# Sparse attention over lists: when the first q rows are normed, where one list tile is loaded and where the first gathers land

## The chip, the cores and the metric

The kernel runs on one core of a Trainium2 chip. The metric is the device time in microseconds (us) of one execution. The engines are named as in the profile: PE (TensorE), DVE (VectorE), ACT (ScalarE), POOL (GpSimd) and SP (SyncE, which here only issues transfers). Each engine takes its instructions in the order in which they stand in its own program.

## The reference

One graph attention layer with 4096 source rows x, 4096 target rows h_target, width 512, 8 heads of 64, and a 4096 x 4096 adjacency matrix of which about 0.4% is set. The masks and scales are ones and the biases zeros in these inputs.

```python
hs = layer_norm(h_source, ln1_scale, ln1_bias)
ht = layer_norm(h_target, ln1_scale, ln1_bias)
q = (ht @ Wq + bq).reshape(T, H, HD) / jnp.sqrt(jnp.float32(HD))
k = (hs @ Wk + bk).reshape(S, H, HD)
v = (hs @ Wv + bv).reshape(S, H, HD)
logits = jnp.einsum('thd,shd->hts', q, k)
logits = jnp.where(edge_mask[None] != 0, logits, NEG)
ctx = jnp.einsum('hts,shd->thd', jax.nn.softmax(logits, axis=-1), v).reshape(T, D)
ht = layer_norm(ht + ctx @ Wo + bo, ln2_scale, ln2_bias)
out = _layernorm(x + ht + jax.nn.gelu(ht @ W1) @ W2)
```

## The kernel before

The kernel uses that few edges are set. It makes, for every target row, a list of the source rows it is joined to, gathers those rows of k and v, and computes attention over the list alone. A second, general path stands behind a flag and isn't taken with these inputs.

**Work and tiles.** Rows go in tiles of 128, so there are 32 tiles of targets and 32 of sources. Four kinds of work are woven together.

- The *projection* (`project`) loads x two tiles at a time into ring slots 12 to 16, norms them on ACT, transposes them on PE, and for every source tile makes k and v (`source`): four matmuls of 128x512 for each half (L929), a copy from PSUM to the buffer `kvr` on ACT for each half (L931), and one write of 128 rows of k|v, 512 KB, to the DRAM table `kvd` (L935, from ACT's queue). For the last source tiles `kvr` is one of ring slots 8 to 10.
- The *lists* (`all_edges`, `edges`) read the adjacency matrix in quarters of 128 x 1024 integers, 512 KB, four to a target tile and 128 in all. I number them from 0: quarter 80 is the first of target tile 20. SP issues the load (L713, `quarter`), ACT turns it into 0/1 bytes and counts them (L728, the sign step), DVE multiplies by positions (L733) and takes maxima (L735). After a tile's fourth quarter DVE decodes the list (L742 to L759), and the candidates that remain are written out from SP (L766). `sort` orders the first 16 tiles' rows by the number of their edges; one step of it on DVE is L849. The sorted records are scattered to DRAM (L853, POOL).
- The *front* of a target tile (`front`) makes its q: POOL has fetched the tile's record (L979, `prefetch`) and gathers its rows of h_target (L966 into `tq`). Then come the tie (L994) and the copy of tags (L997) on DVE, the norm on ACT (L998), four transposes on PE (L1002), four ACT steps (L1005), four matmuls with Wq (L1011) and a DVE step (L1016).
- *Attention* (`attention`) takes up to three list entries at once. POOL gathers 128 rows of k|v for each entry (L966 into `kv`, 512 KB), DVE multiplies by q (L1220) and adds up each head (L1225), ACT takes the exponential (L1229, or L1238 for a tile's first entries), DVE and ACT scale v (L1184, L1204), and PE transposes and accumulates (L1192). A finished tile goes on to the output projection (L1115) and the feed-forward part (`feed`: L1325, L1328, L1334), which fills PE for most of the run.

**The ring.** `ring` has 20 slots of 128 x 4 KB that change their use. While lists are made beside the projection, slots 0 to 7 hold list quarters, quarter n in slot n % 8, for the first NA + FILL = 16 + 5 tiles; 8 to 11 hold rows of h_target (their moments are taken early); 12 to 16 hold x. Slots 17 and 18 are the two "wide" buffers, which take turns: they serve the sort and the list quarters of all later tiles, so a load there waits until the sign step two quarters earlier is done. Slot 19 is scratch. In attention the gathers go round slots 0 to 16 (`place`, worked out when the program is built), later 0 to 19.

**What sets the order.** The Python generators are woven by costs written in the code (`_weave`), and a scheduler then orders each engine's instructions. Since it could place a front early, the tie is a data dependence put there on purpose: L994 reads a column of a tile in the list `latest` and writes the norm factors back unchanged, so that a front can't be placed before that tile is written. For the first fronts (`first_fronts`, two tiles, EARLY = 2) `latest` holds the first column of a `kvr` buffer of projection step n >= 14, that is, of one of the last four source tiles. Later it holds a column of the logits.

The first gather of k|v waits until all of `kvd` is written.

Of the kernel before, what the change touches and what calls it, by code (L numbers as in the profile page):

```python
# [423 lines left out]
def _take(gen, n):  # L424

    for _ in range(n):
        cost = next(gen, StopIteration)
        if cost is StopIteration:
            return
        yield cost  # L430
# [13 lines left out]
def adj_resnorm_kernel(  # L444
# [34 lines left out]
    N, D = x.shape  # L479
# [3 lines left out]
    NT = N // P  # L483
    G = 2
# [3 lines left out]
    NQ = 4  # L488
# [12 lines left out]
    NA, NBT = len(CAPS_A), len(CAPS_B)  # L501
# [31 lines left out]
    with tc.tile_pool(name="keep", bufs=1) as keep:  # L533
# [17 lines left out]
        with ExitStack() as late:  # L551
# [22 lines left out]
            def turn_of(name, places):  # L574
                turns[name] += 1
                return places[turns[name] % len(places)]
# [127 lines left out]
            adjs = []  # L704
            DEEP = 8
            FILL = 5

            def quarter(i, h):
                if i < NA + FILL:
                    a = ring[:, (i * NQ + h) % DEEP, :].bitcast(I32)  # L710
                else:
                    a = turn_of("wide", wide)
                nc.sync.dma_start(a, adj[i * P:(i + 1) * P, h * QW:(h + 1) * QW])  # L713
                return a

            def edges(i):

                part = 1 if i >= NA else 0
                rec = Rs[part][:, i - PARTS[part][0], :]
                cand = lp.tile([P, SEG, 8], U16, name="cand", bufs=2)  # L720
                for h in range(NQ):
                    n = i * NQ + h
                    while len(adjs) < min(n + 2, NT * NQ):
                        adjs.append(quarter(*divmod(len(adjs), NQ)))
                    a, adjs[n] = adjs[n], None

                    sg = turn_of("signs", signs)
                    nc.scalar.activation(sg, a, AF.Sign, accum_out=dpart[:, i, h:h + 1])  # L728
                    ahead = min(n + DEEP - 1, n + 3 + n // 2)
                    while len(adjs) < min(max(n + 3, min(ahead, (NA + FILL) * NQ)), NT * NQ):  # L730
                        adjs.append(quarter(*divmod(len(adjs), NQ)))
                    wd = sg.bitcast(U16)
                    nc.vector.tensor_tensor(wd, wd, lio, ALU.mult)  # L733
                    for s, (w0, w1) in enumerate(SEGS):
                        nc.vector.max(cand[:, h * SQ + s, :], wd[:, w0:w1])  # L735
                    if h == 1:
                        keep_rest()
                    if h % 2 and moms:
                        moments(moms.pop(0))
                    yield 2.0  # L740
                dec = dec_w
                nc.vector.tensor_single_scalar(dec[:, 0], cand, 255, op=ALU.bitwise_and)  # L742
                nc.vector.tensor_single_scalar(dec[:, 1], cand, 8, op=ALU.logical_shift_right)
                gid = lp.tile([P, 2 * SEG, 8], F32, name="gid")
                dec = dec.rearrange("p b s e -> p (b s) e")
                off = segoff.rearrange("p b q s -> p (b q s)")
                nc.vector.scalar_tensor_tensor(gid, dec, 0.0,
                                               off.unsqueeze(2).to_broadcast([P, 2 * SEG, 8]),
                                               op0=ALU.is_gt, op1=ALU.mult)
                nc.vector.tensor_add(gid, gid, dec)  # L750
                flat = gid.rearrange("p s e -> p (s e)")
                for r in range(RE // 8):
                    top = rec[:, E0 + r * 8:E0 + (r + 1) * 8]
                    nc.vector.max(top, flat)
                    if r + 1 < RE // 8:
                        nc.vector.match_replace(flat, top, flat, 0.0)
                held.append((rest_d[i * P:(i + 1) * P, :], flat))
                has = lp.tile([P, MAXE], F32, name="ehas")
                nc.vector.tensor_scalar(has[:, :RE], rec[:, E0:E0 + RE], 0.0, 0.0, op0=ALU.is_gt,  # L759
                                        op1=ALU.add, accum_out=cnt[:, i:i + 1])  # L760
                yield 4.0

            def keep_rest():

                while held:
                    nc.sync.dma_start(*held.pop())  # L766
# [21 lines left out]
            def all_edges():  # L788
                for i in range(NT):
                    yield from edges(i)  # L790
# [9 lines left out]
            def moments(i):  # L800

                while asked and len(asked) > NT - 4 - i:
                    ask(asked.pop(0))
                t = hrow(i)
                stats(ip, t, mvh[:, i, :], "n0")
# [58 lines left out]
            def project(order, t=None):  # L864
# [54 lines left out]
                def source(n, j):  # L919
                    g, hT = order[n], state[n][1]  # L920
                    if asked or moms:
                        kvr = sp.tile([P, 2 * D], F32, name="tq", bufs=3)
                    else:

                        kvr = ring[:, 8 + (n * G + j) % 3, :]
                    for half, w in enumerate((wk, wv)):
                        pkv = psi.tile([P, D], F32, name="pq", bufs=3)
                        for kc in range(KC):
                            nc.tensor.matmul(pkv, hT[:, kc, j * P:(j + 1) * P], w[:, kc, :],  # L929
                                             start=kc == 0, stop=kc == KC - 1)  # L930
                        nc.scalar.copy(kvr[:, half * D:(half + 1) * D], pkv)  # L931
                    if n >= 14:
                        latest[:] = [kvr[:, 0:1]]
                    r0 = 1 + (g * G + j) * P
                    newest[:] = [nc.scalar.dma_start(kvd[r0:r0 + P, :], kvr).ins]  # L935
                    return 7.8
# [26 lines left out]
            recs, tqs, h2Ts, done, ready, latest, newest = {}, {}, {}, set(), [], [], []  # L963
# [6 lines left out]
            def prefetch(i):  # L970
                if i >= NT or i in recs:
                    return
                r0 = TILES[i][0]
                part = 1 if r0 >= PARTS[1][0] * P else 0
                assert part in done
                r0 -= PARTS[part][0] * P
                rec = sp.tile([P, E0 + MAXE], I32, name="rec", bufs=6)

                nc.gpsimd.dma_start(rec[:, :RW], recs_d[part][r0:r0 + P, :])  # L979
                recs[i] = rec  # L980
# [39 lines left out]
            EARLY = 2  # L1020
# [1 line left out]
            SG = [(i, j0, min(S, cap - j0)) for i, (_, cap) in enumerate(TILES)  # L1022
                  for j0 in range(0, cap, S)]
            kvs, rests, fronts = {}, {}, {}
            place = [0]
            for i, _, n in SG:
                if place[-1] + n > RING[i >= NA]:
                    place[-1] = 0
# [6 lines left out]
            def step(gens, i):  # L1035

                if i in gens and next(gens[i], StopIteration) is StopIteration:
                    del gens[i]
# [111 lines left out]
            def go_on():  # L1150
                for i in list(fronts):
                    step(fronts, i)

            def first_fronts():

                for i in range(EARLY):
                    prefetch(i)
                for i in range(EARLY):
                    fronts[i] = front(i)
                    step(fronts, i)  # L1160
                while not latest:
                    yield None
                while fronts:
                    go_on()
                    yield 4.0
# [235 lines left out]
            def prepare():  # L1401

                yield from _take(ed, NA * steps)
                ready.append("lists")
                while moms:
                    moments(moms.pop(0))
                rs, nm = rstd_of(wp, mvh, NT, "n0")
                for R, (i0, n) in zip(Rs, PARTS):
                    Rf = R.bitcast(F32)
                    nc.vector.tensor_copy(Rf[:, :, RST], rs[:, i0:i0 + n])  # L1410
                    nc.vector.tensor_copy(Rf[:, :, RST + 1], nm[:, i0:i0 + n])
                nm = turn_of("wide", wide)
                nc.sync.dma_start(nm[:NT, :P], nodemask.rearrange("(c p) -> c p", p=P))
                nmf = nm.bitcast(F32)[:NT, P:2 * P]
                nc.vector.tensor_scalar(nmf, nm[:NT, :P], 1.0, None, op0=ALU.not_equal)
                nc.vector.tensor_reduce(bad[:NT, 0:1], nmf, AX.X, ALU.max)
                yield from sort(0)
                yield from first_fronts()

            def fill():  # L1420
# [3 lines left out]
                yield 9.0  # L1424
                for cost in _take(ed, FILL * steps):
                    yield cost
# [60 lines left out]
```

## Time and profile before

| | us |
|---|---|
| median of 3 runs | 1821.21 (1814.98 to 1824.7) |
| the profiled execution | 1811.19 |
| its span in the trace | 1809.4 |
| PE busy | 1681.5 (93%) |
| DVE busy | 1435.1 (79%) |
| ACT busy | 1221.1 (67%) |
| POOL busy | 979.8 (54%) |
| last k|v copy (L931) starts | 289.38 |
| first k|v gather (L966) starts | 296.81 |
| first attention product on DVE (L1220) starts | 308.02 |

How to read the views that follow. The page gives each engine's busy time, and the span cut into 40 slices of 45 us, where a digit is a busy share in tenths; PEclk is the clock granted to PE, in tenths of full speed, and DMA the mean busy share of the core's 16 DMA engines. A table of windows gives, for each stretch: its length, the busy us of PE, PEld (weight loads), DVE, ACT and POOL with the number of instructions, then PE's clock, the DMA share and GB/s. A list in order of time gives start, duration, engine, line, operation, output and input, and in brackets how long the engine had been idle and what released it. Such a releaser is inferred: where the engine named had long been done, it was another, often a transfer. For a transfer the duration is that of its issue; its landing is asked for separately. A matmul of 32-bit numbers is two records, so four matmuls show as x8.

### The profile page before, as it was taken

To read this page: it belongs to the slowest core of one execution; us is meant where nothing else is said; L and a number is where in the kernel's file an instruction comes from. 1 tells how busy PE (TensorE), PEld (TensorE's weight loads), DVE (VectorE), ACT (ScalarE), POOL (GpSimd) and SP (SyncE) were. 2 spreads that over 40 slices of the span, in tenths; PEclk is the share of its full clock that TensorE was granted. 3 is DMA by queue.
4 is the path that set the end of the run, shared out by engine and by line. 5 is a ranking of instruction groups with operands and counts; after the bars stand their busy time and mean duration, and the time that the engine had idled before them with its cause. 6 is when DMAs were issued, how large, how long until landed. Compare 5 with 4: busy or idle time off the path is not lost. (4 is left out here: it accounts for less than half of the span.)

```text
span 1809.4 us, 22969 instructions
## 1 busy us (share of the span) xinstructions
PE 1681.5 (93%) x7030; PEld 1101.4 (61%) x7030; DVE 1435.1 (79%) x2660; ACT 1221.1 (67%) x3119; POOL 979.8 (54%) x834
## 2 busy tenths in 40 slices
PE   7989984587999989999999989999999999999997
PEld 3434432465766666676776757666666666666664
DVE  6989886899999837777879989979879797988200
ACT  5767654486997636767768867877777676787211
POOL 1000144666566576667767788877575665663101
PEclk9999996698999999999999999999999999999998
DMA  9999968988887647778879888787776777774000
GB/s 343 370 376 375 344 228 293 405 276 321 294 300 237 230 159 258 240 253 279 281 256 320 288 263 292 252 281 261 242 273 216 255 239 247 247 246 149 18 6 26
DMA packets 140268, 463.26 MB, mean 256 GB/s; under 512 B 16500, under 2 KB 21672, under 8 KB 140136
## 3 DMA queue, kind: packets, MB, share of 16 engines
q0 software_dynamic: 96656, 342.64, 55.9%
q1 hardware_dynamic: 35664, 95.98, 15.0%
q10 hardware_dynamic: 7816, 23.08, 3.3%
q8 instruction: 58, 0.95, 0.2%
q14 instruction: 74, 0.61, 0.1%
HBM read 430.75 MB, written 30.89 MB: 255 GB/s over the span
## 5 line engine op out<-in xcount | busy, mean ns | idle before, releaser
L966 POOL DMA_INDIRECT kv<-kvd,rec x603 | 761.1, 1262 | 366.9 <-PE cps L1192 147.8
L1334 PE MATMUL po<-w,gt 128*128 128x512 f32 x1024 | 466.9, 598 | 10.3 <-ACT gt L1328 10.3
L1325 PE MATMUL pf<-h2T,w 128*128 128x256 f32 (+1 forms) x2176 | 466.5, 368 | 0.0
L1325 PEld LDWEIGHTS pf<-h2T,w 128*128 128x128 f32 x2176 | 389.7, 191 | 64.4 <-issue 19.8
L1220 DVE TENSOR_TENSOR kv<-kv,tq 128x1536 f32<-128x1536 f32 (+2 forms) x211 | 352.0, 1677 | 62.0 <-DMA kv<-kvd,rec 57.9
L1204 ACT ACTIVATE kv<-kv,pa 128x64 f32<-128x64 f32 x1520 | 390.9, 337 | 4.5
L1225 DVE TENSOR_REDUCE lg<-kv 128x24 f32<-128x1536 f32 (+2 forms) x211 | 350.4, 1668 | 1.2
L1334 PEld LDWEIGHTS po<-w,gt 128*128 128x128 f32 x1024 | 189.1, 192 | 207.2 <-issue 195.3
L1192 PE MATMUL cps<-ident,kv 128*128 128x128 f32 x2008 | 267.8, 282 | 47.7 <-DVE kv L1184 40.0
L1192 PEld LDWEIGHTS cps<-ident,kv 128*128 128x128 f32 x2008 | 242.2, 146 | 114.0 <-DVE kv L1184 45.8
L1184 DVE TENSOR_TENSOR kv<-kv,p 128x1024 f32<-128x1024 f32 (+1 forms) x211 | 251.3, 1195 | 23.8 <-ACT p L1229 22.5
L687 POOL TENSOR_TENSOR n_rs<-n_ve,mhalf 128x2 f32<-128x2 f32 (+2 forms) x51 | 48.6, 953 | 326.0 <-DVE n_ve L680 173.0
L728 ACT ACTIVATE kv<-kv 128x1024 uint8<-128x1024 int32 x128 | 134.9, 1055 | 94.5 <-DMA kv<-in_adj_dram 42.9
L1328 ACT ACTIVATE gt<-pf 128x512 f32<-128x512 f32 x128 | 76.3, 597 | 87.4 <-PE pf L1325 84.0
L1328 ACT ACT_TABLE_LOAD x103 | 132.1, 1283 | 1.7
L735 DVE MAX8 cand<-kv 128x8 uint16<-128x103 uint16 (+1 forms) x640 | 132.4, 253 | 0.5
L929 PE MATMUL pq<-wk,h2T 128*128 128x512 f32 x256 | 121.3, 619 | 8.3 <-ACT tq L931 5.7
L1229 ACT ACTIVATE p<-lg 128x24 f32<-128x24 f32 (+2 forms) x179 | 39.1, 218 | 120.5 <-DVE lg L1225 119.7
L1011 PE MATMUL t<-wq,tq 128*128 128x512 f32 x256 | 115.7, 595 | 2.1 <-ACT tq L1005 2.1
L929 PE MATMUL pq<-wv,h2T 128*128 128x512 f32 x256 | 115.4, 593 | 1.8 <-DVE rbc L662 1.0
L1115 PE MATMUL t<-wo,rb 128*128 128x512 f32 x256 | 115.2, 592 | 0.0
L929 PEld LDWEIGHTS pq<-wk,h2T 128*128 128x128 f32 x256 | 49.4, 199 | 65.3 <-issue 50.5
(160 smaller groups left out, 1581.8 us busy)
## 6 DMA issues: line engine op xcount, KB each, us to landing
kv<-in_adj_dram SPq DMA_DIRECT2D x128, 512.0 KB, 7.1
kvd<-tq ACTq DMA_DIRECT2D x24, 512.0 KB, 6.6
kv<-kvd,rec POOLq DMA_INDIRECT x603, 5.9
kv<-in_L_gnn_h_target_dram SPq DMA_DIRECT2D x32, 256.0 KB, 8.0
kv<-in_x_dram SPq DMA_DIRECT2D x15, 512.0 KB, 9.3
rest_d<-gid SPq DMA_DIRECT2D x32, 160.0 KB, 4.7
w<-in_L_gnn_W_dram SPq DMA_DIRECT2D x4, 1024.0 KB, 9.9
kvd<-kv ACTq DMA_DIRECT2D x8, 512.0 KB, 5.2
```

Of the source, the lines that this page charges most:

```text
L728: nc.scalar.activation(sg, a, AF.Sign, accum_out=dpart[:, i, h:h + 1])
L735: nc.vector.max(cand[:, h * SQ + s, :], wd[:, w0:w1])
L929: nc.tensor.matmul(pkv, hT[:, kc, j * P:(j + 1) * P], w[:, kc, :], start=kc == 0, stop=kc == KC - 1)
L966: nc.gpsimd.indirect_dma_start(out=dst, out_offset=None, in_=table[:, :], in_offset=bass.IndirectOffsetOnAxis(ap=idx, axis=0))
L1184: nc.vector.tensor_tensor(v4, v4, p[:, j0:j0 + m, :].unsqueeze(3) .to_broadcast([P, m, H, HD]), ALU.mult)
L1192: nc.tensor.matmul(cps[:, c, :], kv[:, j, D + c * P:D + (c + 1) * P], ident, is_transpose=True, start=j0 + j == 0 and c == 0, stop=j0 + n ...
L1204: newest[:] = [nc.scalar.mul(v, v, pa[:, hd:hd + 1]).ins]
L1220: nc.vector.tensor_tensor(kv[:, :n, :D], kv[:, :n, :D], tq[:, :D].unsqueeze(1).to_broadcast([P, n, D]), ALU.mult)
L1225: nc.vector.tensor_reduce(lg[:, :n, :], kv[:, :n, :D].rearrange("p j (h d) -> p j h d", h=H), AX.X, ALU.add)
L1325: nc.tensor.matmul(pf[:, k, :], w1[(f0 + k) // KC][:, kc, (f0 + k) % KC * P:((f0 + k) % KC + 1) * P], h2T[:, kc, :w], start=kc == 0, stop= ...
L1328: nc.scalar.activation(gt, pf, AF.Gelu_apprx_tanh)
L1334: nc.tensor.matmul(po[j], gt[:, k, j * P:(j + 1) * P], w2[(f0 + k) // KC][:, (f0 + k) % KC, :], start=False, stop=f0 + k == FC - 1, skip_g ...
```

## The change

It has four parts. `latest` is filled only at the last source tile, with the first column of the second half (v) of its `kvr`, so the first fronts are tied to the end of the projection. The constant RINGED = NA + FILL - 1 takes the place of NA + FILL where list quarters are placed and loaded ahead: the quarters of tile 20 (80 to 83) use the two wide buffers instead of ring slots 0 to 3. `place` starts at 11 instead of 0: the first two groups of gathers go to slots 11 to 16 and the third to slots 0 to 2. In `first_fronts` the two loops become one, so that each tile's record is fetched just ahead of the start of its front.

```diff
             DEEP = 8
             FILL = 5
+            RINGED = NA + FILL - 1
 
             def quarter(i, h):
-                if i < NA + FILL:
+                if i < RINGED:
                     a = ring[:, (i * NQ + h) % DEEP, :].bitcast(I32)
                 else:
                     a = turn_of("wide", wide)
...
                     ahead = min(n + DEEP - 1, n + 3 + n // 2)
-                    while len(adjs) < min(max(n + 3, min(ahead, (NA + FILL) * NQ)), NT * NQ):
+                    while len(adjs) < min(max(n + 3, min(ahead, RINGED * NQ)), NT * NQ):
                         adjs.append(quarter(*divmod(len(adjs), NQ)))
...
                         nc.scalar.copy(kvr[:, half * D:(half + 1) * D], pkv)
-                    if n >= 14:
-                        latest[:] = [kvr[:, 0:1]]
+                    if n * G + j == NT - 1:
+                        latest[:] = [kvr[:, D:D + 1]]
...
             kvs, rests, fronts = {}, {}, {}
-            place = [0]
+            place = [11]
             for i, _, n in SG:
...
                 for i in range(EARLY):
                     prefetch(i)
-                for i in range(EARLY):
                     fronts[i] = front(i)
                     step(fronts, i)
```

## The prediction

> **What bounds the kernel now.** I read the page's busy table and its 40 slices first, then a table of windows, then each engine's list in order of time between 240 and 320 us, and last the landing times of single transfers.
>
> ```profile
> PE 1681.5 (93%) x7030; PEld 1101.4 (61%) x7030; DVE 1435.1 (79%) x2660; ACT 1221.1 (67%) x3119; POOL 979.8 (54%) x834
> ...
> PE   7989984587999989999999989999999999999997
> ...
> PEclk9999996698999999999999999999999999999998
> DMA  9999968988887647778879888787776777774000
> ```
>
> PE is the bound, with one hole: slices 6 to 8 (271 to 407 us), between the k|v projection and full attention. The windows give its size:
>
> ```profile
> 260.00:280.00 20.00, 11.77 (x28) 5.61 (x27) 9.65 (x45) 6.19 (x11) 11.21 (x14) 0.74 0.64 194
> 280.00:300.00 20.00, 12.26 (x28) 4.86 (x26) 12.02 (x52) 11.02 (x23) 2.58 (x3) 0.92 0.74 240
> 300.00:320.00 20.00, 2.82 (x12) 2.42 (x12) 13.74 (x24) 6.83 (x21) 14.86 (x15) 0.50 1.00 387
> 320.00:340.00 20.00, 8.66 (x32) 6.29 (x32) 17.05 (x24) 7.12 (x28) 12.70 (x10) 0.50 1.03 402
> ...
> 440.00:1750.00 1310.00, 1278.47 (x5635) 878.63 (x5636) 1056.01 (x1362) 936.11 (x2496) 830.74 (x686) 0.99 0.72 240
> ```
>
> From 440 us PE is busy 97.6% of the time, so what starts attention earlier by some microseconds ends the kernel earlier by about as much, unless it is lost before 440. From 300 to 340 the DMA share is full: the gathers themselves set the pace. Before 300 it is 0.64 and 0.74, so there is room. The lists in order of time show who waits in the hole (start, duration, work, idle time before it and its releaser):
>
> ```profile
> 268.84 0.22 DVE L994 SCALAR_TENSOR_TENSOR rec<-rec,kv 128x2 f32<-128x2 f32 x1 [6.78 <-DMA rec<-rec]
> ...
> 273.06 0.81 ACT L998 ACTIVATE tq<-tq,rec 128x512 f32<-128x512 f32 x1 [9.30 <-DVE gid L750]
> ...
> 273.93 1.11 PE L1002 MATMUL t<-ident,tq 128*128 128x128 f32 x4 [7.91 <-ACT tq L998]
> ...
> 289.38 0.62 ACT L931 COPY kv<-pq 128x512 f32<-128x512 f32 x1
> 290.03 0.33 ACTq L935 DMA_DIRECT2D kvd<-kv  x1
> ...
> 296.81 0.96 POOL L966 DMA_INDIRECT kv<-kvd,rec  x1 [20.42 <-ACT kv L728]
> ...
> 308.02 1.77 DVE L1220 TENSOR_TENSOR kv<-kv,tq 128x1536 f32<-128x1536 f32 x1 [1.98 <-DMA kv<-kvd,rec]
> ...
> 314.89 2.82 PE L1192 MATMUL cps<-ident,kv 128*128 128x128 f32 x12 [22.14 <-DVE kv L1184]
> ```
>
> The first two q fronts stand in the middle of the projection. Their tie (L994) waits for records, their ACT step (L998) for the tie and a gather; behind L998 stand five k|v copies (L931), behind L1002 the last row's 16 k|v matmuls. The last copy ends at 290.0, its write lands 6.0 us after issue, at 296.05, and the first gather follows at 296.81. The 20.42 us put down to L728 are not a wait for a slot: slots 0 to 2 held list quarters 80 to 82, whose signs ended by 248.7. The releaser is the k|v write.
>
> **What the skill says.** "Trainium Kernel Development and Optimization", Key Constraints: DMAs from SP, ACT and POOL share the same 16 DMA engines and interleave. The trace agrees: with list loads, weights and gathers together, a gather's landing grows from 7.3 us (issued 296.8) to 16.9 (issued 319.3). "DMA: Bandwidth & Descriptors", Anatomy of one DMA: 2.0 us plus bytes/436e3, which estimates 3.2 us for a 512 KB list quarter. The trace has 3.8 at best and 5.5 as median of 235 to 300 us; I use the trace. "TensorE: Matmul & The Clock Gate", Part 1: the clock is halved after an idle window of about 3.4 us. It agrees: 0.50 from 300 to 340.
>
> **The tie moved.** No instruction but two ACT table loads (1.28 us each, on an engine 67% busy) is added: nothing. In the built order the last row's matmuls stand ahead of both L1002 groups, all copies ahead of L998, and L994 behind the sign step of quarter 92. The 9.30 us on ACT, 7.91 on PE and 6.78 on DVE go. But fourteen sign steps still stand among the copies as before, quarters 79 to 92, and the last copy still stands behind quarter 92. So the list loads decide when the last copy runs.
>
> **The fifth list tile outside the ring.** Quarters 80 to 83 now use the two wide slots. Quarter 81 waits on SP for the sort's L849, as quarter 85 did before (issued 242.27, landed 3.8 later); the rest-of-list writes and loads behind it on SP wait too. From 82 on each load waits for the sign step two quarters earlier. Quarter 81 is signed at 246.5 to 247.6 as before, 80 ends at 246.6, so 82 is issued at 246.7 and 83 at 247.8. Then the even chain 82, 84, ... 92 has six landings and five turns of 1.35 us (sign 1.06, accumulator 0.19, issue 0.1). Landings before: 3.8, 6.3, 4.6 as given, and 5.4, 5.0, 4.0 where a sign step waited for its load: mean 4.85. The three with two loads in flight average 5.6. I take 5.2: 246.7 + 6 x 5.2 + 5 x 1.35 = 284.65; sign 1.06, copy 0.57: the last copy ends at 286.3, not 290.0. PE isn't later: the last half row needs the copy three halves before, due near 272.6, and ends near 276. DVE needs 1.34 us for a quarter (0.41 + 0.93) and 4.1 for a tile's decoding, 2.4 a quarter against 3.3 of the loop.
>
> **The first gathers.** Write issued 286.4, landing 5.5 (before: 4.3, 5.2, 6.0), 0.75 to the first gather: 292.6 against 296.81. The third is issued 2.5 later and lands after 8.2 as before: 303.3, so L1220 starts at 303.8 against 308.02, 4.2 earlier. Slots 11 to 13 instead of 0 to 2 give nothing, as shown above; the cover is the write's landing. Ahead of them on POOL stand two gathers of x that need L997's tags. These move from 274 to about 287 and 288, still 4 us before the k|v gathers; if the copy were much later they would move with it.
>
> **The fronts.** Tie and tags end at 287.1; L998 twice to 288.7; eight transposes to 290; L1005, eight at 0.36, to 291.7; L1011, 7.13 for both, first tile done at 294; L1016 behind a list quarter on DVE at 294.5. All of it, some 8 us, is hidden by the gathers' flight until 303.3, with 8.8 to spare. Without that cover it would cost up to 8.
>
> **First softmax.** Before, L1225 ended at 311.85 but the exponential waited until 313.38, since ACT first signed quarter 98 (312.32). In the new order only quarters up to 96 stand ahead of it; 96 lands near 302. With the second L1016 (0.6) in between, L1225 ends at 307.8 and L1238 follows: 5.5 earlier.
>
> **What comes back.** Two list quarters fewer are done ahead of the first softmax; the built order catches up at about the 17th gather group, at 385 to 400 us of the old trace. That is 2 x 1.34 + half a decode of 4.1 = 4.7 us of DVE, 2.5 of ACT, 1 MB of loads. DVE waits 7 us for gathers from 300 to 345, which can hide it, but from 380 to 400 it is 19.56 of 20 busy. Bounds 0 and 4.7; I take half, 2.3. POOL once waits for a prefetched record (landing 5.6 us, two issues before it), where it later waited 3.3 and 3.6 for PE: nothing. The ring's reuse distance stays 5 to 7 groups: nothing.
>
> **Sum.** 5.5 - 2.3 = 3.2 us earlier: the profiled execution's 1811.2 (span 1809.4) would become 1808.0. That execution lies 10 below the median shown, 1821.2; the same 3.2 from the median gives 1818.
>
> **The rivals.**
> Likeliest, as above, with loads landing in 4.4 to 6.6 us: between 8 faster and 8 slower, 1813 to 1829. Chance 0.58. For it: the last copy is merely moved from one waiting chain to another.
> *Faster*: the loads land in 4.2 on average, since no pair is held up by the record scatters that ended at 263.5. The chain is 6.0 shorter, and the deferred quarters hide in DVE's waits: 5.5 + 6.0 = 11.5 faster, less a little for the full DMA engines: 1811. For it 3.8, 4.0 and 4.6; against it 6.3 with two in flight. Chance 0.22.
> *Slower*: the two-slot loop becomes the bound of the projection's end. At 7.0 us a landing the last copy ends at 297.1, the gathers start 6.6 later than before, the softmax some 5.3 later, and the deferred quarters cost all 4.7: 10.0 slower, 1831. With 2.3 for them the loss begins at 5.7 us; with 4.7 it passes 0.5% at 6.85. For it: medians of 6.3 from 240 to 330 us and 7.4 once gathers run; against it: DMA shares of 0.54 to 0.74 in that stretch. Chance 0.20.
> That the slots change nothing is already in the likeliest case. If the wait named L728 had been a real slot wait, the write at 296.05 would still hold the gathers.
>
> **How the numbers follow.** 0.5% of 1821 is 9.1 us, about what a measurement of this kernel can tell from no change. Faster by more: 0.22. Slower by more: 0.20. Within: 0.58. The time is the likeliest case's 1818; its own range is 1813 to 1829. From 1808 to 1831 it takes in most of both other cases and leaves the outer parts, 2 in 10 with the runs' own spread (1815 to 1825).
>
> **What would show it.** Right: no ACT stall ahead of L998 but short ones ahead of L728; PE goes from L929 to L1002 without projection behind it; last L931 near 286; first k|v gather near 292 to 293; first L1220 near 304; first L1192 near 309. Wrong: the last copy at 290 or later with L728 waiting for list loads (the slower case), or before 281 (the faster one); an L1016 that ends after the gathers have landed; DVE list work between 380 and 400 ahead of an idle PE.

## The result

The changed kernel takes 1817.42 us in the median (1813.57 to 1822.71), the kernel before 1818.92 (1810.74 to 1824.7), 20 executions of each on one chip. The ratio is 0.9994, with a 95% interval of 0.9983 to 1.0005: no difference that the runs can show, and the 1818 that was predicted. The profiled execution after the change took 1817.49 us (span 1815.5).

The page of the changed kernel, busy times and slices as in the prediction:

```profile
PE 1677.8 (92%) x7030; PEld 1097.9 (60%) x7030; DVE 1436.5 (79%) x2660; ACT 1224.1 (67%) x3121; POOL 982.2 (54%) x834
...
PE   7989984597999979999999989999999999999997
...
PEclk9999996698999989999999999999999999999998
DMA  9999968989887557777878878787776776774000
```

The hole in slices 6 to 8 stands on PE at 4, 5 and 9 tenths, where it stood at 4, 5 and 8. The table of windows says how it moved inside (length, busy us of PE, PEld, DVE, ACT, POOL, then PE's clock, DMA share, GB/s):

```profile
260.00:280.00 20.00, 13.92 (x31) 5.83 (x32) 12.22 (x51) 8.82 (x17) 8.91 (x12) 1.00 0.75 231
280.00:300.00 20.00, 7.97 (x17) 3.93 (x16) 11.55 (x52) 11.75 (x25) 4.93 (x5) 0.57 0.78 246
300.00:320.00 20.00, 7.11 (x22) 3.97 (x21) 13.26 (x19) 6.91 (x22) 15.38 (x15) 0.74 1.02 398
320.00:340.00 20.00, 5.64 (x24) 4.84 (x24) 14.47 (x23) 4.71 (x18) 12.09 (x10) 0.51 1.03 402
```

PE's busy time over the four windows is 34.64 us, where it was 35.51. The order changed as predicted. The lists of the changed kernel in order of time (the lines between 708 and 1158 have one number more than before; L995 is the old L994, L932 the old L931, and so on):

```profile
266.11 0.58 ACT L932 COPY kv<-pq 128x512 f32<-128x512 f32 x1 [3.95 <-remote]
...
288.93 1.06 ACT L729 ACTIVATE kv<-kv 128x1024 uint8<-128x1024 int32 x1 [2.57 <-DMA kv<-in_adj_dram]
...
289.99 0.57 ACT L932 COPY kv<-pq 128x512 f32<-128x512 f32 x1
...
291.03 1.52 ACT L999 ACTIVATE tq<-tq,rec 128x512 f32<-128x512 f32 x2 [0.48 <-DVE rec L995]
...
291.90 1.97 PE L1003 MATMUL t<-ident,tq 128*128 128x128 f32 x8 [11.28 <-ACT tq L999]
...
296.58 0.94 POOL L967 DMA_INDIRECT kv<-kvd,rec  x1 [3.00 <-DMA rest_d<-gid]
...
308.06 1.76 DVE L1220 TENSOR_TENSOR kv<-kv,tq 128x1536 f32<-128x1536 f32 x1 [5.18 <-DMA kv<-kvd,rec]
...
313.65 2.82 PE L1192 MATMUL cps<-ident,kv 128*128 128x128 f32 x12 [9.36 <-issue]
```

The long wait ahead of the norm (L999) is gone, and ahead of the last copies stand short waits for list loads at the sign steps (L729). On PE the wait wasn't removed but moved: 11.28 us ahead of L1003, at a place where PE has nothing else to do. Yet the last copy starts at 289.99 (before 289.38) and the first product at 308.06 (before 308.02): in this execution attention starts when it always did. So two questions were open. Why did the start stay, and would an earlier start have been worth anything?

### The profile page after: what moved, and what is told of

Its sections match the earlier page's. It is cut to its first block, busy times and chain, and to the rows that moved or that the text cites. A ratio compares the mean times of both kernels' runs of the same rounds, so it can differ in the third digit from the quotient of the medians.

```text
span 1815.5 us, 22973 instructions
## 1 busy us (share of the span) xinstructions
PE 1677.8 (92%) x7030; PEld 1097.9 (60%) x7030; DVE 1436.5 (79%) x2660; ACT 1224.1 (67%) x3121; POOL 982.2 (54%) x834
## 5 line engine op out<-in xcount | busy, mean ns | idle before, releaser
L1325 PE MATMUL pf<-h2T,w 128*128 128x256 f32 (+1 forms) x2176 | 465.9, 368 | 0.1
L1325 PEld LDWEIGHTS pf<-h2T,w 128*128 128x128 f32 x2176 | 389.3, 191 | 64.5 <-issue 20.3
L1220 DVE TENSOR_TENSOR kv<-kv,tq 128x1536 f32<-128x1536 f32 (+2 forms) x211 | 351.6, 1675 | 68.3 <-DMA kv<-kvd,rec 56.2
L1225 DVE TENSOR_REDUCE lg<-kv 128x24 f32<-128x1536 f32 (+2 forms) x211 | 350.1, 1666 | 1.4
L729 ACT ACTIVATE kv<-kv 128x1024 uint8<-128x1024 int32 x128 | 134.9, 1056 | 100.0 <-DMA kv<-in_adj_dram 51.7
```

The source lines that it names most:

```text
L1220: nc.vector.tensor_tensor(kv[:, :n, :D], kv[:, :n, :D], tq[:, :D].unsqueeze(1).to_broadcast([P, n, D]), ALU.mult)
L1225: nc.vector.tensor_reduce(lg[:, :n, :], kv[:, :n, :D].rearrange("p j (h d) -> p j h d", h=H), AX.X, ALU.add)
L1325: nc.tensor.matmul(pf[:, k, :], w1[(f0 + k) // KC][:, kc, (f0 + k) % KC * P:((f0 + k) % KC + 1) * P], h2T[:, kc, :w], start=kc == 0, stop= ...
```

## The experiments

Every ratio is to the kernel before, run on the same chip beside it. The table holds what the experiments turn on: from each profile the start of attention's first product on DVE (L1220), the start of the multiplication that ends the first tile's sums (L1103 before, L1104 after, `rb<-cps,rb`), and PE's busy time between 260 and 440 us.

| kernel | first product | first tile's sums | PE busy, 260 to 440 | ratio (95% interval) |
|---|---|---|---|---|
| before | 308.02 | 351.40 | 117.97 | 1 |
| the change | 308.06 | 351.16 | 117.75 | 0.9994 (0.9983 to 1.0005) |
| tie alone | 304.00 | 350.13 | 118.75 | 0.9996 (0.9981 to 1.0010) |
| fifth tile alone | 308.02 | 354.20 | 116.77 | 1.0016 (1.0001 to 1.0031) |
| slots alone | 307.45 | 351.54 | 116.95 | 1.0029 (1.0016 to 1.0042) |
| tie and fifth tile | 307.63 | 349.86 | 119.39 | 0.9989 (0.9975 to 1.0003) |
| tie and slots | 306.08 | 351.77 | 113.21 | 1.0070 (1.0049 to 1.0091) |
| change, sign step held | 292.19 | 337.00 | 119.45 | 1.0001 (0.9986 to 1.0016) |
| change, late weights | 303.71 | 335.73 | 125.21 | 0.9993 (0.9979 to 1.0008) |
| tie and fifth tile, late weights | 303.67 | 335.53 | 123.73 | 0.9956 (0.9942 to 0.9971) |
| change, held, late weights | 287.51 | 320.98 | 134.85 | 0.9935 (0.9914 to 0.9956) |
| tie, fifth tile, held, late weights | 292.27 | 324.78 | 130.78 | 0.9924 (0.9895 to 0.9954) |

### The parts one by one

The tie alone, on the kernel before:

```diff
-                    if n >= 14:
-                        latest[:] = [kvr[:, 0:1]]
+                    if n * G + j == NT - 1:
+                        latest[:] = [kvr[:, D:D + 1]]
```

> The kernel before with the tie moved alone: tile 20 stays in the ring, gathers start at slot 0. Theory (the list loads that stand ahead of the last k|v copies decide when those end): the two-slot loop starts four quarters later, at 84, and quarter 93 is the last ahead of the copy, so the last copy ends near 284, not 290, the first gather near 290 to 291, the first L1220 near 302, and since 99 sign steps still stand ahead of the first exponential, as before, nothing is put off: 4 to 7 us faster than before, ratio 0.9965 to 0.998. Rival (the gathers wait for slots 0 to 2, as the 20.42 us put down to L728 say): the first gather stays at 296 to 297 though the copy is earlier, and the time is that of before within 2 us.

The last copy started at 287.00, the first gather at 293.99 and the first product at 304.00, 4.0 us earlier than before. The time didn't follow: 0.9996. The first tile's sums came only 1.3 us earlier.

The sign step of quarter 84 held back, in the changed kernel, until the last k|v write has been issued, so that no list work of tile 21 and later stands among the copies:

```diff
-            adjs = []
+            adjs, written = [], []
...
-                    nc.scalar.activation(sg, a, AF.Sign, accum_out=dpart[:, i, h:h + 1])
+                    with ExitStack() as hold:
+                        if (i, h) == (21, 0):
+                            hold.enter_context(tc.issue_after(written[0]))
+                        nc.scalar.activation(sg, a, AF.Sign, accum_out=dpart[:, i, h:h + 1])
...
+            written.append(newest[-1])
             src.close()
             mid.close()
```

> The changed kernel, with the sign step of quarter 84 held back until the last k|v write is issued, so that no quarter after 84 stands ahead of a copy (85 signs instead of 93). Theory: the copies then wait for PE alone; the last one ends near 277 to 279, the first gather starts near 284 to 286, the first L1220 near 295 to 297. Nine quarters fewer are signed before the first exponential, some 21 us of DVE work put off. If an earlier start of attention were all that counts: 10 us faster than the changed kernel. Rival (what counts is DVE's list and attention work together up to about 440 us, not where attention starts): the start is 11 us earlier and the time within 4 us of the changed kernel or slower.

```profile
277.18 0.59 ACT L935 COPY kv<-pq 128x512 f32<-128x512 f32 x1 [2.85 <-PE pq L933]
...
281.37 0.94 POOL L970 DMA_INDIRECT kv<-kvd,rec  x1 [0.77 <-issue]
...
292.19 1.76 DVE L1223 TENSOR_TENSOR kv<-kv,tq 128x1536 f32<-128x1536 f32 x1 [5.03 <-DMA kv<-kvd,rec]
...
337.00 0.69 DVE L1107 TENSOR_TENSOR rb<-cps,rb 128x512 f32<-128x512 f32 x1
```

In this list in order of time (three lines more than in the changed kernel) the last copy waits for PE, not for a list load, and attention's first product stands 15.9 us earlier than in the changed kernel. The time is the same, 1.0001. This is the clearest run of the study: a start of attention that is 16 us earlier is worth nothing here. The traces show where the 16 us go. The multiplications that end the sums of the first four tiles start at 337.0, 364.6, 406.6 and 441.7 us with the held step, and at 351.2, 372.0, 414.8 and 440.9 in the changed kernel: the lead is 14 us at the first tile, 7 and 8 at the next two, and gone at the fourth (later tiles of this execution are 3 to 7 us ahead again, its end 2; in the times nothing is left). The list work that was put off is done in between: 91 quarters had been signed by 340 us, against 99 in the changed kernel, and 102 by 400 us in both. And in that stretch DVE has no room for it. The windows from 340 to 440, the changed kernel and the one with the held step:

```profile
340.00:440.00 100.00, 83.10 (x448) 61.09 (x448) 98.38 (x178) 73.31 (x216) 66.27 (x55) 0.89 0.92 332
```

```profile
340.00:440.00 100.00, 81.10 (x420) 59.16 (x419) 100.00 (x233) 75.10 (x200) 61.13 (x50) 0.85 0.90 332
```

DVE is busy 98.38 and 100.00 of 100 us. (The DMA share, 0.92 and 0.90, is full only up to 360 and from 420 us.) Over the whole 180 us from 260 to 440 it was busy 149.88 in the changed kernel and 148.13 here, and PE 117.75 and 119.45: by 440 both had done about as much as if attention had started late.

The fifth list tile alone (RINGED, in the kernel before), and the first slots alone:

```diff
+            RINGED = NA + FILL - 1
```

> The kernel before with the fifth list tile on the wide buffers and nothing else. Theory: the old tie still stalls ACT near 264 to 273, and the two-slot loop now starts at quarter 80; 91 signs stand ahead of the last copy, 96 ahead of the first exponential. Last copy near 289 to 292, first gather near 296 to 299: equal to before or up to 4 us slower. Rival (slots): gathers no longer wait for quarters of tile 20 and start at or before 295: up to 3 us faster.

```diff
-            place = [0]
+            place = [11]
```

> The kernel before with place = [11] and nothing else; the order on ACT is the same up to the first exponentials. Theory: no wait for a slot existed, so the first gather stays at 296 to 297.5 and the time within 2 us of before. Rival (slots): the first gather comes earlier, down to the landing of the last k|v write, and the wait put down to the sign step shrinks from 20.42 us by more than 2.

The fifth tile alone gives 1.0016, some 3 us slower. The slots alone give 1.0029, 5 us slower and not within the 2 us that were expected, though the first gather (297.05, before 296.81) and the first product (307.45) stand where they stood. So the slots do nothing to the start, as predicted, but they are not free.

### Do the parts add up?

The ring begun at slot 0 in the changed kernel leaves the tie and the fifth tile; RINGED = NA + FILL in the changed kernel leaves the tie and the slots.

> The tie and the fifth tile without the new first slots (the changed kernel with the ring begun at slot 0). If the parts' times add up, the new slots cost what they cost alone (0.29%, 5 us): 5 us faster than the changed kernel, ratio to the kernel before 0.9955 to 0.9975. If what each part does to the time is only how the later instructions fall into order on POOL, parts don't add up: ratio 0.9985 to 1.0015.

> The tie and the new first slots, with the fifth list tile inside the ring as before. If the parts' times add up: 0.9996 and 0.29%, ratio 1.0015 to 1.0035. If they don't: 0.9985 to 1.0015. The start of attention by both: as with the tie alone, first product about 304 us.

They don't. The slots cost 0.29% alone, 0.74% beside the tie (1.0070 against 0.9996), and beside the tie and the fifth tile 0.05%, which can't be told from nothing. Neither of the two simple readings holds: the tie and the slots together are slower than both allowed for. In that kernel the list of waits on DVE from 340 to 440 us (total, times, longest) has a line that the changed kernel doesn't have in that stretch:

```profile
DVE kv L1220 <- DMA kv<-kvd,rec: 10.6, 3, 5.4
```

PE's busy time to 440 is 113.21 instead of 117.75, so part of its loss lies there. Each edit reorders later instructions on all engines, beside the slots themselves, and no run separates order from slots. The cause of the slots' cost stays open.

### Does DVE set the end of the list stretch?

From 340 to 580 us DVE is busy 236.57 of 240 us in the changed kernel. Two runs give it more work, once inside this stretch and once behind it. Nothing is left out of the computation.

```diff
-                    for s, (w0, w1) in enumerate(SEGS):
-                        nc.vector.max(cand[:, h * SQ + s, :], wd[:, w0:w1])
+                    for s, (w0, w1) in enumerate(SEGS + (SEGS if i >= 25 and h % 2 else [])):
+                        nc.vector.max(cand[:, h * SQ + s % len(SEGS), :], wd[:, w0:w1])
```

> The changed kernel in which, of the last seven target tiles of the lists (tiles 25 to 31), every second quarter takes its five eight-largest instructions on DVE twice over, with the same outcome: 7 x 2 x 5 = 70 more instructions of 0.251 us, 17.6 us of DVE's time more, all between about 400 and 575 us. Theory A (between 340 and 580 us DVE has list and attention work without a gap, and this sum, not the start of attention, sets when that stretch ends): 12 to 18 us slower than the changed kernel, ratio to the kernel before 1.006 to 1.0095. Theory B (the prediction's premise: TensorE's work laid from the start of attention sets the end, DVE keeps up): 0 to 3 us slower, ratio 0.999 to 1.001.

```diff
+                            if 14 <= i < 24 and j0 == 0:
+                                nc.vector.tensor_reduce(lg[:, :n, :],
+                                                        kv[:, :n, :D].rearrange("p j (h d) -> p j h d", h=H),
+                                                        AX.X, ALU.add)
```

> The changed kernel in which the sum over the head dimension (L1225) is taken twice, with the same outcome, for the first piece of attention tiles 14 to 23: ten more DVE instructions of 1.75 us, 17.5 us more, all between about 960 and 1420 us, where DVE is busy 407 of 460 us and TensorE 440. Theory A (the place matters: DVE sets the end only in the list stretch): 0 to 5 us slower than the changed kernel, ratio to the kernel before 0.999 to 1.0025. Rival C (DVE's work counts everywhere, so the amount of DVE work in the kernel is what sets its time): 12 to 18 us slower, ratio 1.006 to 1.0095.

The pages show what was added, DVE's total in the first run and in the second:

```profile
PE 1685.0 (93%) x7030; PEld 1102.1 (61%) x7030; DVE 1447.2 (80%) x2730; ACT 1222.8 (67%) x3119; POOL 982.6 (54%) x834
```

```profile
PE 1678.7 (93%) x7030; PEld 1097.2 (61%) x7030; DVE 1451.8 (80%) x2670; ACT 1224.4 (68%) x3121; POOL 972.6 (54%) x834
```

Beside the changed kernel's 1436.5 that is 10.7 and 15.3 us more. The first is less than the 17.6 expected, since the 70 instructions overlap: five of them in a row take 0.93 us and not five times 0.251, and ten take 1.76.

The first run gives 1.0046 (1.0029 to 1.0063), the second 1.0022 (1.0010 to 1.0033). Against the changed kernel's 0.9994 that is 9.4 us, give or take 3.7, for 10.7 of added work, and 5.1, give or take 2.9, for 15.3. Theory B falls with the first run and rival C with the second. Theory A holds: in the list stretch DVE's work counts with most or all of its time, and the 12 to 18 us that were expected were too many because the added work was priced too high. Behind it, with DVE 407 of 460 us busy, it counts with about a third.

### The transfers between 300 and 360

The DMA share is full from 300 to 360 us: 1.03 at 402 GB/s in the changed kernel, 24.12 MB in all. Of what is loaded there, 4.19 MB are the last four weight loads of the feed-forward part, issued at 312.49 to 323.48 and first needed at about 390, when PE starts the third of the first tile's four blocks (L1325). The next runs issue them later:

```diff
                 for q, pool in enumerate(pools):
-                    yield 10.0
+                    yield 60.0 if q == 0 else 15.0
                     with tc.issue_after(newest[-1]):
```

> The changed kernel with the last four weight loads (L586/L587, 1,024 KB each, 4.19 MB in all, issued on ACT's queue at 314 to 325 us, first used at about 390) issued some 40 us later. Theory D (from about 300 to 360 us the DMA engines are full, share 1.03 at about 403 GB/s, so the bytes ahead of a gather and not the start of attention set when the first tiles end): 4.19 MB / 0.403 MB per us = 10.4 us of transfers leave that stretch; first tile's product with its sums (L1104, 351.2 in the changed kernel) 6 to 10 us earlier; TensorE idle from 290 to 380 us down from 39 by 5 to 10; end 2 to 8 us earlier than the changed kernel, ratio to the kernel before 0.995 to 0.9983. Theory A (DVE's lists and attention from 340 to 580 set it): the first tile may end earlier, the end 0 to 2 us, ratio 0.9983 to 0.9995.

> The same late weights in the kernel whose sign of quarter 84 is held behind the last k|v write, where attention began 16 us earlier and the end stayed (ratio 1.0001). Theory D (the earlier start was lost because the DMA engines were full): with 10.4 us of transfers gone from the stretch a part of the 16 us stays: ratio 0.993 to 0.998. Theory A: 0.9985 to 1.0005.

> The same late weights in the kernel with the tie and the fifth tile and the ring begun at slot 0 (ratio 0.9989 without them). Theory D: ratio 0.9945 to 0.9978. Theory A: 0.998 to 0.9995.

What the loads did is plain in the list of DVE's instructions in order of time. First the changed kernel, where pieces of the first tile wait for their gathers up to 337 us:

```profile
308.06 1.76 DVE L1220 TENSOR_TENSOR kv<-kv,tq 128x1536 f32<-128x1536 f32 x1 [5.18 <-DMA kv<-kvd,rec]
...
318.33 1.76 DVE L1220 TENSOR_TENSOR kv<-kv,tq 128x1536 f32<-128x1536 f32 x1 [0.34 <-DMA kv<-kvd,rec]
...
329.64 1.76 DVE L1220 TENSOR_TENSOR kv<-kv,tq 128x1536 f32<-128x1536 f32 x1 [3.17 <-DMA kv<-kvd,rec]
...
337.04 1.76 DVE L1220 TENSOR_TENSOR kv<-kv,tq 128x1536 f32<-128x1536 f32 x1 [2.36 <-DMA kv<-kvd,rec]
...
351.16 0.68 DVE L1104 TENSOR_TENSOR rb<-cps,rb 128x512 f32<-128x512 f32 x1
```

Then the changed kernel with late weights, where only the first two pieces wait, the second hardly:

```profile
303.71 1.76 DVE L1220 TENSOR_TENSOR kv<-kv,tq 128x1536 f32<-128x1536 f32 x1 [4.90 <-DMA kv<-kvd,rec]
...
309.53 1.76 DVE L1220 TENSOR_TENSOR kv<-kv,tq 128x1536 f32<-128x1536 f32 x1 [0.29 <-DMA kv<-kvd,rec]
...
335.73 0.68 DVE L1104 TENSOR_TENSOR rb<-cps,rb 128x512 f32<-128x512 f32 x1
```

From the first product to the first tile's sums it took 43.4 us before, 43.1 after the change and 44.8 with the held step. With late weights it takes 32.0, 33.5 and 31.9 in the three kernels, some 11 us less. That looks like the 10.4 us which 4.19 MB take at 0.402 MB per us, but only a part of it is waiting. The windows between the two marks, the changed kernel without and with late weights:

```profile
308.06:351.16 43.10, 14.83 (x66) 13.23 (x67) 36.94 (x47) 17.92 (x67) 27.77 (x22) 0.54 1.03 405
```

```profile
303.71:335.73 32.02, 14.35 (x65) 12.12 (x66) 31.73 (x33) 16.77 (x62) 25.73 (x20) 0.59 1.02 404
```

DVE's idle time falls from 6.2 us to 0.3, and its work from 36.94 to 31.73, because in the new order fewer list steps and one product fewer stand ahead of the first tile's sums. So about 6 of the 11 us are waits for gathers that the weights had held up, and about 5 are another order of the same work. The weights did stand in the way. Once they are gone, DVE is busy all the time and sets the pace of the first tile, though the DMA share there is still 1.02.

On the time the three runs differ. In the changed kernel late weights alone give 0.9993, nothing, as the theory of a full DVE had it. With the held step they give 0.9935 (12 us), and with the tie and the fifth tile 0.9956 (8 us), as the theory of full DMA engines had it. The windows from 260 to 440 of four kernels, in this order the changed one, that with the held step, that with late weights, and that with both:

```profile
260.00:440.00 180.00, 117.75 (x540) 79.66 (x540) 149.88 (x321) 105.49 (x296) 107.58 (x94) 0.81 0.91 326
```

```profile
260.00:440.00 180.00, 119.45 (x550) 82.38 (x549) 148.13 (x315) 108.56 (x300) 109.39 (x95) 0.80 0.88 328
```

```profile
260.00:440.00 180.00, 125.21 (x560) 84.03 (x560) 155.84 (x331) 108.84 (x309) 109.25 (x98) 0.80 0.91 335
```

```profile
260.00:440.00 180.00, 134.85 (x609) 92.31 (x607) 155.55 (x330) 118.72 (x326) 115.01 (x99) 0.83 0.91 342
```

PE's column: 1.7 us more by 440 for the held step, 7.5 for late weights, 17.1 for both. But busy time isn't work: a matmul at half the clock is busy twice as long, and the granted clock is 0.80 to 0.83 here. Counted in the columns that PE's matmuls had moved by 440 us (every record with its own width), the held step is 3,072 ahead of the changed kernel, late weights 2,560 and both together 16,512. At the pace of the projection before (a half of k|v, 4,096 columns, every 3.44 us) that is 2.6, 2.1 and 13.9 us. So most of the 7.5 us is slower clock. Neither edit alone brings much by 440, both together bring a lot, as the times say: 1.0001, 0.9993 and 0.9935.

With the tie and the fifth tile it is otherwise. There late weights alone are worth 6 us (0.9956 against 0.9989), at 2,432 columns more by 440, about 2 us. That kernel differs from the changed one in the first slots alone, and why late weights help only there isn't explained. Part may be the draw: the profiled execution of the changed kernel with late weights took 1808.0 us, the second fastest of 14, whose median is 1811.42.

The last run takes the new slots out of the kernel with the held step and late weights:

> The tie, the fifth tile, the held sign of quarter 84 and the late weights, with the ring begun at slot 0: the previous best (ratio 0.9935) without the new first slots. If the new slots cost here what they cost in the kernels with the tie, the fifth tile and late weights (0.9993 against 0.9956, 0.37%): ratio 0.9885 to 0.9915. If that cost is a matter of the order that each whole program happens to get: 0.992 to 0.996.

It gives 0.9924 (0.9895 to 0.9954), which can't be told from 0.9935; the 0.37% by which the slots slowed the kernel with late weights alone (0.9993 against 0.9956) isn't there. Both beat the two kernels of the change: 1801.08 and 1802.43 us, where the kernel before took 1813.54 and 1813.77 beside them.

## Why the prediction was right, and where not

**The start of attention.** The prediction had the last copy at 286, the first gather at 292.6 and the first product at 303.8; its profile shows 289.99, 296.58 and 308.06. Six profiled executions share one order on ACT up to the last copy: the change, its two variants with doubled work, its late weights, and the tie with the fifth tile, with and without late weights. Their last copies start at 289.99, 285.37, 287.49, 285.55, 288.10 and 285.22 (mean 286.95), their first products at 308.06, 303.68, 305.94, 303.71, 307.63 and 303.67 (mean 305.45). Against those means the forecast is 1 to 2 us early. The profile of the changed kernel drew the latest of six, at the edge of the prediction's own sign of being wrong (a last copy at 290 or later behind list loads). Its loop from quarter 82 to the sign of 92 took 42.2 us, not 38. The term that was off is a wait that the sum didn't have: 3.95 us on ACT ahead of the copy at 266.11, put down to no engine. It is 1.5 and 2.2 us in the executions with 287.49 and 288.10 and absent in the three that end near 285.4. What it waits for isn't settled. The list loads of that profile took 5.7 us from issue to the start of the sign step, in the mean of eight (4.7 to 8.8), where 5.2 was taken. The longest, quarter 83, isn't a landing by the trace, which names no load ahead of that step (256.56); without it the mean is 5.2. The 3.2 us of the Trainium skill's fit ("DMA: Bandwidth & Descriptors", Anatomy of one DMA) are far off; the page gives that fit for transfers issued from POOL, and the list loads are issued from SP.

**The tie and its stalls.** Right: L999 waits 0.48 us, the fronts follow the last copy, and no projection stands behind them. The fronts were hidden as said, with 7.2 us to spare instead of 8.8 (first L1017 at 300.89): their matmuls with Wq took 9.68 us, not 7.13, since PE's clock was halved from 282.7 to 299.8, after its wait. The prediction named that halving and didn't price it here. The work behind the old L1002 was eight matmuls, not 16: the 16 are records, two to a matmul. The two x gathers ran at 291.15 and 292.63, 4 us ahead of the k|v gathers, and delayed nothing.

**First softmax.** The exponential followed L1225 without quarter 98 between them, at 312.11 instead of 313.38. That is 1.3 us earlier and not 5.5, since the product itself came no earlier.

**The step that failed** is the premise under the sum: "what starts attention earlier by some microseconds ends the kernel earlier by about as much, unless it is lost before 440". Nearly all of it is lost before 440. The tie alone starts attention 4 us earlier and the held step 16, and neither moves the time. With the tie alone 1.3 of 4.0 us are left at the first tile's sums, in the stretch of which the prediction had said that "the gathers themselves set the pace". With the held step 14.2 of 15.9 are left there (337.00 against 351.16) and none at the fourth tile: the list work put off comes back where DVE is full. The prediction had a term for this, 0 to 4.7 us with 2.3 taken, and saw DVE full from 380 to 400; DVE is full from 340, and where more list work is put off the term grows to the whole gain. For the change itself, with two quarters put off, 3.2 us earlier was predicted and by the ratio 1.1 measured (between 3.1 earlier and 0.9 later). Its profile gives no earlier start, so its own time says nothing on what an earlier start is worth; the tie alone and the held step do.

That the predicted time fits so well is in part luck. A gain of 3.2 us lies just outside the interval measured, and the kernel before itself ran 2.3 us faster beside the changed one than in the median that the prediction started from. Taken from 1818.92, the same 3.2 us would have given 1815.7.

**The slots.** Right that they do nothing to the first gathers. "The ring's reuse distance stays 5 to 7 groups: nothing" was wrong as a price: alone they cost 0.29%. In the changed kernel it isn't seen; in the kernels with late weights it is seen once (0.37%) and not once the step is held.

**The rivals.** The slower one, landings of 7 us in the two-slot loop, didn't occur: 5.7 us, or 5.2 without quarter 83, lie at or below the 5.7 from which it was to lose. The faster one, landings of 4.2, didn't occur either, and the held step speaks against its gain too: there the last copy was at 277.18, before the 281 that it named, and the time stayed.

## What to carry to other kernels

Before passing an earlier start on to the end, count how much work the bounding engine has done at the point where it becomes full (here the columns PE's matmuls moved by 440 us; its busy time also grows when its clock falls). If a full engine lies between, as DVE does here from 340 us, the start can move 16 us and that count by less than 3. Ask of every transfer in a stretch with full DMA engines when it is first needed; here four weight loads, issued over 70 us before their first use, made DVE wait some 6 us in the first tile. Two stretches in series, one bound by transfers and one by an engine, can each hide the gain from the other, as in the changed kernel: lift both in one run before calling either worthless. Price added work by what it adds to the engine's busy time, and compare a span between two marks only where the same work stands between them.

## What was not expected of the hardware

Gathers and loads from DRAM together kept 399 GB/s in the kernel before, 402 in the changed one and 404 with the held step over the 60 us from 300 to 360, on one core alone. The Trainium skill's page "DMA: Bandwidth & Descriptors", section Where 436 GB/s comes from, gives 435 for the ports and about 358 as the limit of the memory for one core, and says that the latter binds, though it also names a measured 425; in these traces the 358 does not bind.

PE's clock fell after shorter waits than the 3.4 us of the page "TensorE: Matmul & The Clock Gate", Part 1. Four matmuls of 128x512 (eight records) take 3.70 us with their start. In the 14 traces of this case, the first 20 us of each left out, 43 such groups follow a wait of 1.0 to 1.95 us, and all took 3.70. Of 53 that follow one of 1.95 to 3.4 us, 37 took 5.1 to 6.7 us; the others took 3.70, in the changed kernel after 2.25 and 3.04 us. The page calls its window free-running, so that a wait can fall anywhere in it, but a wait of 2 us doesn't fill it. Where page and traces differ here, the traces decide: a wait of PE of 2 us or more often cost some 1.7 us beside itself.

In the six kernels that share one order on ACT, attention started up to 4.4 us apart, and one kernel's times lie up to 15 us apart. A step of a few us read from a single pair of profiles, as at the last copy here, is within that.
